# Cross attention of a decoder layer: probabilities turned in 32x32 blocks on VectorE, value products of two token tiles on sixteen 32x32 tiles of TensorE

## The chip, the core and the metric

The kernel runs on one core of a Trainium2 chip, as one launch. The metric is the device time of that launch in microseconds (us), smaller is better. The engines are named as in the profile: PE is TensorE (PEld its weight loads), DVE is VectorE, ACT is ScalarE, POOL is GpSimd and SP is SyncE, which issues the DMAs. Each engine works through its own queue in order.

## What is computed

A small encoder runs over a context of 77 positions, and its output is the memory of a decoder layer over 2 batches of 2048 tokens, width 512, 16 heads of 32. The decoder layer has causal self-attention, cross attention to the 77 positions and a feed-forward part of width 2048. All is fp32. The change touches cross attention:

```python
q = (xq @ wq.T + bq)          # 2048 tokens x 512, 16 heads of 32
scores = einsum('bhqd,bhkd->bhqk', q, k) / sqrt(32) + bias   # k: 77 positions
attn = softmax(scores, axis=-1)
out = einsum('bhqk,bhkd->bhqd', attn, v)                     # 32 values a head
y = y + out.reshape(B, T, 512) @ w_out.T + b_out
y = y + relu(ln(y) @ ff1.T + b1) @ ff2.T + b2
```

## The kernel before

The 4096 tokens are cut into 8 blocks of 512 tokens, and a block into four tiles of 128 tokens. The kernel first runs the encoder and the decoder's self-attention, and the cross attention of block 0 with it (`first_cross`, L888). The rest, whose first L1638 comes at 1652.9 us, is a loop (L1950) over the eight blocks. For each block it has 56 slots (`per`, L1500), and in each slot it issues two things in this order: one step of the cross attention of the *next* block (`next(side)`, the generator `cross`, L1727), then one step of this block's feed-forward part (`ff_slot`, L1704). The order of the work is thus written out by hand. The lists `plan[n]` hold what `cross` issues in slot n, and every engine takes its share of it in that order.

**Feed-forward part.** Slots 0 to 27 make the first product (`first_product`, L1629, matmuls L1638: eight PE instructions of 256 columns in each slot). Slots 28 to 55 make the second (`second_product`, L1658, matmuls L1667: sixteen PE instructions of 128 columns in a slot, and eight in each fourth slot). Both products use a scheme with seven products in place of eight, on two levels in the second. Its sums and differences of quarter matrices are made by DVE and POOL: `sums_h` (L1595, with `half_sum` L1584; the subtractions are recorded at L962, the additions at L1587 and L1605) runs four slots ahead of the product that reads them, in slots 24 to 51. Its product number j (order `TWO`, L1490) needs them in slots 28+4j and after; number 3 reads the sum called S4, number 4 the one called S3. Two parts of the product put their results together on DVE (L1676, and L1681 to L1683) and add them to y on POOL (L1687).

**Cross attention of a block** (`cross`). Slots 0 to 7: layer norm of the four tiles (`norm_stages`, L785: statistics on DVE L793 to L795 and POOL L796 and L797, centring on ACT L803, four transposes on PE L811, four copies on ACT L814). Slots 9 to 12: the queries (L1758). Then for each of the four tiles `attend_stages` (L824), begun in slots 13, 18, 23 and 28:

- `score` (L831), at once: sixteen products of 32 contracted rows with 77 positions (L836) into four PSUM banks; DVE then takes the maximum (L845) and subtracts it (L846), a pair for each bank, and writes the scores to SBUF.
- `exp` (L848), 2 slots on, on ACT (L849); `sums` (L851), 3 slots on, on DVE (L854, L855); `normalize` (L858), also 3 slots on, on POOL (L860).
- `turned` (L862), 7 slots on: sixteen PE transposes of 128 x 77 (L866) into four banks, each copied by ACT (L867).
- `times_v` (L869), 11 slots on: sixteen products with contraction 77 and 32 output rows (L874), four at a time on PE's four column groups, into one bank that ACT copies (L878).

After the second tile of a pair, `sums_o` (L1782) makes the differences for the output projection of that pair, and `o_product` (L1790, matmuls L1801) makes its seven products in slots 31 to 34 and 40 to 43; DVE adds each to y (L1805). A last layer norm (`n3`, same functions) begins in slots 35, 36, 44 and 45. An fp32 matmul is two MATMUL records and two weight loads in the profile, a transpose is one of each.

Four PSUM banks (0 to 3) go round in a ring among these cross steps (`bank`, L180); the feed-forward part has the other four. The probabilities of a tile lie in `prs[t % 2]`, 16 heads x 77 side by side; the two buffers are in `oT_all` and in `pts_all[5:8]`. The values of a batch lie once, 77 x 512, in a tile that was loaded before (`last_loads`, L1370, and `next_batch`, L1815).

Of the kernel before, what the change touches and what calls it, by code (L numbers as in the profile page):

```python
# [10 lines left out]
F32 = mybir.dt.float32  # L11
AF = mybir.ActivationFunctionType
ALU = mybir.AluOpType
# [4 lines left out]
P = 128  # L18
B, T, S, D = 2, 2048, 77, 512
H, HD, DFF = 16, 32, 2048  # L20
NC = D // P
# [33 lines left out]
def tile_encoder_decoder(ctx: ExitStack, tc: tile.TileContext, ins, out):  # L55
# [103 lines left out]
    with (  # L159
# [20 lines left out]
        def bank():  # L180

            ring.append(ring.pop(0))
            return psum[:, ring[-1], :]
# [6 lines left out]
        def rows4(r):  # L190
            return slice(r * HD, (r + 1) * HD)
# [626 lines left out]
        def q_group(o, w, nT, dst):  # L818
# [2 lines left out]
                nc.tensor.matmul(mm, w[:, c, :], nT[:, c, :], start=(c == 0), stop=(c == NC - 1))  # L821
            nc.vector.tensor_scalar(dst, mm, vec("dec_ca_in_b", o), SCALE, ALU.add, ALU.mult)

        def attend_stages(q, kTc, v, y, biased, pr, pts, place, w_o, bi=None):  # L824


            prh = pr.rearrange("p (h k) -> p h k", k=S)
            by_r = pr.rearrange("p (g r k) -> p g r k", r=HC, k=S)
            keep = {}

            def score():  # L831
# [14 lines left out]
                    nc.vector.tensor_tensor(d, s, mx[:, :, r, None].to_broadcast([P, NC, S]), ALU.subtract)  # L846

            def exp():  # L848
                nc.scalar.activation(pr, pr, AF.Exp)  # L849

            def sums():  # L851
                su = sm.tile([P, H], F32, name="csu", tag="csu", bufs=2)
# [108 lines left out]
        def minus(engine, out, a, b):  # L961
            engine.tensor_tensor(out, a, b, ALU.subtract)  # L962
# [385 lines left out]
        n2_sums, o_sums, vc, qT = [high[:, (4 + k) * D : (5 + k) * D] for k in range(4)], [], [], []  # L1348

        def big(i):  # L1350
            return vflat[:, i * TB * D : (i + 1) * TB * D]
# [375 lines left out]
        def cross(x):  # L1727
# [44 lines left out]
            plan[8].append(lambda: [sum_n(n, of_n2) for n in ("T1", "T2")])  # L1772
            plan[9].append(lambda: [sum_n(n, of_n2) for n in ("T3", "T4")])

            def of_o(t, name):
                if name[0] == "S":
                    i = int(name[1]) - 1
                    return o_sums[i // 2][:, ts(i % 2, TOK)]
                r, c = int(name[0]) - 1, int(name[1]) - 1
                return held["o", t + r]["oT"][:, ts(c, TOK)]  # L1780

            def sums_o(t):  # L1782
                s = {n: of_o(t, n) for n in ("S1", "S2", "S3", "S4", "11", "12", "21")}
                a21, a22 = (held["o", t + 1]["bank"][:, ts(c, TOK)] for c in range(2))
                minus(ve, s["S3"], s["11"], a21)
                minus(ve, s["S2"], a22, s["S3"])
                ve.tensor_tensor(s["S1"], s["21"], a22, ALU.add)
                minus(gp, s["S4"], s["12"], s["S2"])

            def o_product(t, j):  # L1790
                if j == 0:
                    held["out"] = bank(), bank()
                name, by, chain, fresh, to = ONE[j]
                a, mm = of_o(t, name), held["out"][chain][:, :TOK]
                if by[0] == "T":
                    w = next_w(2)
# [8 lines left out]
                ve.tensor_tensor(d, d, mm, ALU.add)  # L1805
# [1 line left out]
            for n, js in Q_SLOTS.items():  # L1807
                plan[n].append(lambda js=js: [q_product(j) for j in js])
            for n, js in O_SLOTS.items():
                t = 0 if n < 36 else 2  # L1810
                plan[n].append(lambda t=t, js=js: [o_product(t, j) for j in js])
            bias_1 = None
            if m == 0:

                def next_batch():  # L1815
                    nc.sync.dma_start(kTc, ckT_d[:, :, ts(b, S)])
                    nc.sync.dma_start(vc[0][:S, :], cv_d[:, b, :])

                plan[1].append(next_batch)

                spare = [y_of(x + 1, r) for r in range(HC)]
                bias_1 = [a[:, : NC * S].rearrange("p (g k) -> p g k", k=S) for a in spare]
                plan[3].append(lambda: bias_tile(prs[0].rearrange("p (h k) -> p h k", k=S), 2, P, S, 255))
                plan[5].append(lambda: [bias_tile(a, 2, P, S, 255 - P, r, HC) for r, a in enumerate(bias_1)])
            for t in range(TB):
                at = 13 + 5 * t
                y = lambda t=t: y_of(x, t)
                biased = m == 0 and t < 2
                fs = attend_stages(
                    lambda g, t=t: qT[g // 2][:, g % 2, ts(t, P)], kTc, vc[0][:S, :], y, biased, prs[t % 2],  # L1830
                    lambda g: pts_all[:S, g, :], place("xr"), wbt,
                    bias_1 if biased and t else None,
                )
                held["o", t] = fs[7]
# [159 lines left out]
```

## Time and profile before

| what | number |
|---|---|
| median of 3 runs | 2726.36 us (2726.09 to 2729.47) |
| profiled execution, first to last instruction | 2726.8 us |
| one block with cross attention, as in the loop (window 2215.2 to 2352.2 us of the trace) | 137.0 us |
| the last block, without cross attention (window 2626.2 to 2720.4 us) | 94.2 us |
| granted TensorE clock, mean | 0.997 of full speed |

The profiled execution has no time of its own beside its span: the span is 2726.8 us, and the median of the runs is 0.4 us below it. A page of the profile gives the busy time of each engine; the chain of waits is the work that ended last, followed back from the end. In the timeline, neighbouring instructions of one line are merged into a row (start, length, engine, line, count); in the windows, a row gives each engine's busy time in a stretch. A matmul's record runs on after the next one has started, so the cost of a burst on PE is read from its start to the next line's start.

### The profile page before, as it was taken

The numbers are of one execution on the slowest core, as the hardware profiler recorded it, in microseconds if no ns is written. First come the engines' busy times: TensorE is split into PE (matmuls) and PEld (weight loads), VectorE is DVE, ScalarE is ACT, GpSimd is POOL, SyncE is SP. The second block draws the span as 40 slices with busy tenths as digits, with TensorE's granted clock in tenths as the row PEclk, the third lists the DMA queues.
The fourth block names the chain that finished last, engine by engine and source line by source line (L and its number), as shares of the span: only waits on it lengthen the run. The fifth ranks groups of instructions, "written<-read, shape, count | busy, mean of one in ns | idle before, by whom it ended". The sixth has DMA issues, their size and how long they took to land.

```text
span 2726.8 us, 68267 instructions
## 1 busy us (share of the span) xinstructions
PE 2708.1 (99%) x26606; PEld 2217.9 (81%) x26606; DVE 1839.9 (67%) x5445; ACT 1537.0 (56%) x2978; POOL 1002.4 (37%) x844
## 2 busy tenths in 40 slices
PE   9999999999999999999999999999999999999998
PEld 6678877777876677777777777898989898989898
DVE  4776688888885677788888783646464746464645
ACT  3554567777786547667777784444444444444431
POOL 2612235500300513322300203455556565656456
PEclk9999999999999999999999999999999999999999
DMA  8724355511213522343311206565657565656465
GB/s 242 213 92 135 126 155 164 168 50 43 67 45 89 143 76 72 111 133 98 126 50 35 79 19 220 171 214 173 213 171 239 168 216 170 218 166 219 151 224 185
DMA packets 296277, 385.10 MB, mean 141 GB/s; under 512 B 41184, under 2 KB 165648, under 8 KB 295826
## 3 DMA queue, kind: packets, MB, share of 16 engines
q1 hardware_dynamic: 295954, 380.73, 44.1%
q8 instruction: 211, 3.46, 0.5%
q14 instruction: 112, 0.92, 0.1%
HBM read 334.15 MB, written 46.47 MB: 140 GB/s over the span
## 4 chain that ended last, share of the span: by engine, by line
PE 95%; DVE 1%; ACT 1%; DMA 1%; POOL 1%; issue 1%; SPq 0%; DVEq 0%; POOLq 0%; ACTq 0%
PE psum L427 18%; PE psum L1638 14%; PE psum L1667 13%; PE psum L375 11%; PE psum L456 9%; PE psum L1134 8%; PE psum L1801 3%; PE psum L1758 3%; PE psum L1049 3%; PE psum L866 2%; PE psum L836 1%; PE psum L874 1%; PE psum L590 1%; PE psum L811 1%; PE psum L239 1%; PE psum L215 1%
## 5 line engine op out<-in xcount | busy, mean ns | idle before, releaser
L406 ACT ACTIVATE pp<-pp,nm 128x128 f32<-128x128 f32 (+15 forms) x512 | 611.8, 1200 | 28.6 <-DVE nm L401 27.8
L384 DVE TENSOR_SCALAR_CACHE_REDUCE pp<-psum 128x512 f32<-128x512 f32 (+3 forms) x1024 | 556.2, 591 | 51.3 <-PE psum L375 49.7
L434 ACT COPY pts<-psum 128x512 f32<-128x512 f32 x714 | 384.1, 594 | 312.6 <-PE psum L427 265.6
L427 PE MATMUL psum<-ident,pp 128*128 128x128 f32 x4352 | 530.4, 277 | 4.7 <-ACT nT L310 4.0
L427 PEld LDWEIGHTS psum<-ident,pp 128*128 128x128 f32 x4352 | 474.0, 141 | 55.7 <-DVE pp L384 21.4
L375 PE MATMUL psum<-kT,q 32*128 32x512 f32 (+3 forms) x2560 | 336.5, 559 | 2.5 <-DVE q L217 1.0
L456 PEld LDWEIGHTS psum<-pts,vv 128*32 128x32 f32 x8704 | 226.4, 110 | 127.4 <-DVE pp L384 55.4
L1667 PE MATMUL psum<-pp 128*128 128x128 f32 x2560 | 304.5, 276 | 1.9 <-POOL pp L962 1.6
L1667 PEld LDWEIGHTS psum<-pp 128*128 128x128 f32 x2560 | 296.3, 192 | 8.6 <-issue 2.8
L432 DVE COPY pts<-psum 128x512 f32<-128x512 f32 x374 | 245.2, 685 | 82.6 <-PE psum L427 80.3
L456 PE MATMUL psum<-pts,vv 128*32 128x128 f32 x8704 | 279.6, 276 | 0.8 <-DVE mx L391 0.3
L962 POOL TENSOR_TENSOR pp<-pp 128x512 f32<-128x512 f32 x159 | 212.8, 1356 | 111.0 <-DMA pp<-in_dec_ff_wT_dram 50.6
L1638 PE MATMUL psum<-vv,pp 128*128 128x256 f32 x1024 | 236.2, 381 | 0.0
L375 PEld LDWEIGHTS psum<-kT,q 32*128 32x128 f32 x2560 | 146.3, 183 | 107.1 <-issue 41.3
L1638 PEld LDWEIGHTS psum<-vv,pp 128*128 128x128 f32 x1024 | 190.3, 190 | 25.8 <-issue 0.5
L391 DVE CUSTOM_DVE_ANT_0 pp<-psum,bias 128x256 f32<-128x256 f32 (+1 forms) x512 | 196.0, 411 | 19.7 <-PE psum L375 19.7
L1651 DVE TENSOR_TENSOR kT<-kT,psum 128x512 f32<-128x512 f32 x96 | 65.8, 686 | 191.6 <-PE psum L1638 191.4
L1654 ACT ACTIVATE kT<-kT,vecs 128x256 f32<-128x256 f32 x192 | 86.9, 501 | 156.6 <-DVE kT L1651 155.9
L1638 PE MATMUL psum<-nT,pp 128*128 128x256 f32 x768 | 174.1, 380 | 0.5 <-DVE oT L471 0.5
L1638 PEld LDWEIGHTS psum<-nT,pp 128*128 128x128 f32 x768 | 144.2, 190 | 20.8 <-issue 1.4
L1675 ACT COPY oT<-psum 128x128 f32<-128x128 f32 x56 | 15.0, 268 | 238.9 <-PE psum L1667 238.9
L494 POOL TENSOR_TENSOR oT<-rirows,oT 128x512 f32<-128x512 f32 x30 | 38.4, 1280 | 293.6 <-DMA rirows<-rec 181.7
(272 smaller groups left out, 4110.6 us busy)
## 6 DMA issues: line engine op xcount, KB each, us to landing
pp<-w_d SPq DMA_DIRECT2D x520, 256.0 KB
pp<-in_dec_ff_wT_dram SPq DMA_DIRECT2D x112, 256.0 KB
bias<-tzg SPq DMA_DIRECT2D x128, 128.0 KB
pp<-wo_d SPq DMA_DIRECT2D x56, 256.0 KB
wqk<-in_dec_sa_in_wT_dram SPq DMA_DIRECT2D x52, 256.0 KB
wqk<-sa_q SPq DMA_DIRECT2D x84, 128.0 KB
vv<-in_enc_ff_wT_dram SPq DMA_DIRECT2D x8, 1024.0 KB
xr<-in_x_dram SPq DMA_DIRECT2D x32, 256.0 KB
```

The source lines that it names most:

```text
L375: nc.tensor.matmul(banks[r][:, : kn * P], q[rows4(r), ts(t, P)], kT[rows4(r), g, k0 * P : (k0 + kn) * P], start=True, stop=True,)
L384: nc.vector.tensor_scalar(p[:, k0 : k0 + far], s[:, :far], 1.0, None, ALU.mult, ALU.max, accum_out=st["mx"][:, r, c : c + 1],)
L391: nc.vector.tensor_tensor_reduce(p[:, k0 + far : i + 1], s[:, far:kn], near[:, 2 - (kn - far) :], 1.0, LOWEST, ALU.add, ALU.max, accum_out ...
L406: nc.scalar.activation(p, p, AF.Exp, bias=nm, accum_out=to)
L427: nc.tensor.transpose(pt[:, ts(x, P)], state[n]["p"][r][:, k], ident)
L432: nc.vector.tensor_copy(pts[:, : len(load), :], pt[:, :w])
L434: nc.scalar.copy(pts[:, : len(load), :], pt[:, :w])
L456: nc.tensor.matmul(ot[rows4(r)], vv[:, k, ts(g * HC + r, HD)], got.pop((n, k, r)), start=k == k0 and (whole or not begun), stop=k == k1 - ...
L962: engine.tensor_tensor(out, a, b, ALU.subtract)
L1134: nc.tensor.matmul(mm[:, ts(f, TOK)], left[:, c, ts(f, P)], right[:, c, :], start=c == 0, stop=c == 1,)
L1638: nc.tensor.matmul(mm[:, ts(f, TOK)], a[:, c, ts(f, P)], b[:, c, :], start=fresh and f == 0 and c == 0, stop=c == 1, skip_group_check=True,)
L1667: nc.tensor.matmul(psum[:, bank_i, ts(col, P)], lhs[:, c, :], w[:, c, :], start=fresh and k in (0, 3) and c == 0, stop=c == 3, skip_group_ ...
```

## The change

Transposes on PE and their copies on ACT go away. VectorE turns the normalised probabilities in place, each 32x32 block by itself (`blocks_turned`). For that each head gets 96 columns instead of 77 (three blocks of 32), and both probability buffers move to `oT_all`; `mixed` of the feed-forward part moves to `pts_all[5:8]`. After the turn, a block has 32 positions on 32 partitions and 32 queries on its columns, and the four groups of 32 partitions hold the four groups of 32 queries. The products with the values are therefore made for each of the four row groups, with the values lying four times (`v4`, 32 positions on each group, three chunks of positions, the rest of the last chunk zero). `times_v` now does two tiles at once: 4 groups of heads x 3 chunks x 4 row groups x 4 column groups = 192 matmuls with 32 contracted rows, 32 output rows and 64 columns, into four banks; two ACT copies bring the result into the old order, one for each tile.

The slots move: scores begin in 13, 17, 31 and 35 (13, 18, 23 and 28 before), the turn comes 6 slots after a tile's score, the products of a pair 8 slots after its second tile's score (25 and 43), the output products in 27 to 30 and 45 to 48, the last norms in 31, 32, 49 and 50. `first_cross` uses `attend_stages` as before.

```diff
+        def heads_of(pr):
+            return pr.rearrange("p (h k) -> p h k", h=H)[:, :, :S]
...
-            prh = pr.rearrange("p (h k) -> p h k", k=S)
-            by_r = pr.rearrange("p (g r k) -> p g r k", r=HC, k=S)
+            prh = heads_of(pr)
+            by_r = prh.rearrange("p (g r) k -> p g r k", r=HC)
...
-                nc.scalar.activation(pr, pr, AF.Exp)
+                nc.scalar.activation(prh, prh, AF.Exp)
...
-        prs = [oflat[:, : H * S], pts_all[:, 5:8, :].rearrange("p a k -> p (a k)")[:, : H * S]]
+        KC = 3
+        prs = oflat.rearrange("p (a x) -> p a x", a=2)
+        v4 = pts_all[:, :KC, :]
...
-            t = sb.tile([P, MB], F32, name="q", tag="q", bufs=3)
-            nc.sync.dma_start(t[:S, :], cv_d[:, 0, :])
-            vc.append(t)
...
-        O_SLOTS = {at + k: js for at in (31, 40) for k, js in enumerate(((0, 1), (2, 3), (4, 5), (6,)))}
+        SCORE_AT = (13, 17, 31, 35)
+        OUT_AT = (27, 45)
+        NORM_AT = (31, 32, 49, 50)
+        O_SLOTS = {at + k: js for at in OUT_AT for k, js in enumerate(((0, 1), (2, 3), (4, 5), (6,)))}
...
-        mixed = oflat[:, H * S : H * S + 12 * P].rearrange("p (k n) -> p k n", n=P)
+        mixed = pts_all[:, 5:8, :].rearrange("p a (k n) -> p (a k) n", n=P)
...
+            def load_v(batch):
+                for a in range(P // RB):
+                    for c in range(KC):
+                        n = min(RB, S - c * RB)
+                        nc.sync.dma_start(v4[a * RB : a * RB + n, c, :], cv_d[c * RB : c * RB + n, batch, :])
+
+            def first_v():
+                nc.gpsimd.memset(v4[:, KC - 1, :], 0.0)
+                load_v(0)
+
+            def blocks_turned(t):
+                pr = prs[:, t % 2]
+                nc.vector.transpose(pr, pr)
+
+            def times_v(t):
+                for _ in range(P // RB):
+                    bank()
+                pT = prs.rearrange("p a (h c q) -> p a h c q", h=H, c=KC)
+                for g in range(NC):
+                    for c in range(KC):
+                        for a in range(P // RB):
+                            for r in range(HC):
+                                h = g * HC + r
+                                nc.tensor.matmul(
+                                    psum[rows4(r), a, ts(g, 2 * RB)], v4[ts(a, RB), c, ts(h, HD)],
+                                    pT[ts(a, RB), :, h, c, :], start=(c == 0), stop=(c == KC - 1),
+                                )
+                got = psum[:, : P // RB, : NC * 2 * RB].rearrange("p a (g x q) -> p x g a q", g=NC, x=2)
+                for x in range(2):
+                    oT = place("xr")()
+                    nc.scalar.copy(oT.rearrange("p (g a q) -> p g a q", g=NC, q=RB), got[:, x])
+                    held["o", t + x] = oT, got[:, x]
+                sums_o(t)
...
-                minus(ve, s["S3"], s["11"], a21)
-                minus(ve, s["S2"], a22, s["S3"])
-                ve.tensor_tensor(s["S1"], s["21"], a22, ALU.add)
+                f = {n: s[n].rearrange("p (g a q) -> p g a q", g=2, q=RB) for n in ("S1", "S2", "S3", "11", "21")}
+                minus(ve, f["S3"], f["11"], a21)
+                minus(ve, f["S2"], a22, f["S3"])
+                ve.tensor_tensor(f["S1"], f["21"], a22, ALU.add)
...
+            if x == 1:
+                plan[10].append(first_v)
...
-                    nc.sync.dma_start(vc[0][:S, :], cv_d[:, b, :])
+                    load_v(b)
...
             for t in range(TB):
-                at = 13 + 5 * t
+                at = SCORE_AT[t]
...
-                if t % 2:
-                    fs = fs[:5] + (lambda t=t, f=fs[5]: [f(), sums_o(t - 1)],)
-
-                for k, f in zip((0, 2, 3, 3, 7, 11), fs):
-                    plan[at + k].append(f)
+                fs = fs[:4] + (lambda t=t: blocks_turned(t),)
+                for k, f in zip((0, 2, 3, 3, 6), fs):
+                    plan[at + k].append(f)
+                if t % 2:
+                    plan[at + 8].append(lambda t=t: times_v(t - 1))
                 fs = norm_stages(y, "n3", bo, place("xt"), lambda t=t: nTt[:, :, ts(t, P)])
-                at = (35, 36, 44, 45)[t]
+                at = NORM_AT[t]
```

More of the change, by code (lines that the diff above doesn't have):

```diff
@@ L1345, in tile_encoder_decoder @@
         oflat = oT_all.rearrange("p a q -> p (a q)")
-        prs = [oflat[:, : H * S], pts_all[:, 5:8, :].rearrange("p a k -> p (a k)")[:, : H * S]]
+        KC = 3
+        prs = oflat.rearrange("p (a x) -> p a x", a=2)
+        v4 = pts_all[:, :KC, :]
         kTc = pts_all[:, 4, : NC * S].rearrange("p (c k) -> p c k", k=S)
-        n2_sums, o_sums, vc, qT = [high[:, (4 + k) * D : (5 + k) * D] for k in range(4)], [], [], []
+        n2_sums, o_sums, qT = [high[:, (4 + k) * D : (5 + k) * D] for k in range(4)], [], []
         def big(i):
@@ L1779, in of_o @@
                 r, c = int(name[0]) - 1, int(name[1]) - 1
-                return held["o", t + r]["oT"][:, ts(c, TOK)]
+                return held["o", t + r][0][:, ts(c, TOK)]
             def sums_o(t):
                 s = {n: of_o(t, n) for n in ("S1", "S2", "S3", "S4", "11", "12", "21")}
-                a21, a22 = (held["o", t + 1]["bank"][:, ts(c, TOK)] for c in range(2))
-                minus(ve, s["S3"], s["11"], a21)
-                minus(ve, s["S2"], a22, s["S3"])
-                ve.tensor_tensor(s["S1"], s["21"], a22, ALU.add)
+                a21, a22 = (held["o", t + 1][1][:, 2 * c : 2 * c + 2] for c in range(2))
+                f = {n: s[n].rearrange("p (g a q) -> p g a q", g=2, q=RB) for n in ("S1", "S2", "S3", "11", "21")}
+                minus(ve, f["S3"], f["11"], a21)
+                minus(ve, f["S2"], a22, f["S3"])
+                ve.tensor_tensor(f["S1"], f["21"], a22, ALU.add)
                 minus(gp, s["S4"], s["12"], s["S2"])
@@ L1809, in cross @@
             for n, js in O_SLOTS.items():
-                t = 0 if n < 36 else 2
+                t = 0 if n < OUT_AT[1] else 2
                 plan[n].append(lambda t=t, js=js: [o_product(t, j) for j in js])
+            if x == 1:
+                plan[10].append(first_v)
             bias_1 = None
@@ L1822, in cross @@
                 bias_1 = [a[:, : NC * S].rearrange("p (g k) -> p g k", k=S) for a in spare]
-                plan[3].append(lambda: bias_tile(prs[0].rearrange("p (h k) -> p h k", k=S), 2, P, S, 255))
+                plan[3].append(lambda: bias_tile(heads_of(prs[:, 0]), 2, P, S, 255))
                 plan[5].append(lambda: [bias_tile(a, 2, P, S, 255 - P, r, HC) for r, a in enumerate(bias_1)])
             for t in range(TB):
-                at = 13 + 5 * t
+                at = SCORE_AT[t]
                 y = lambda t=t: y_of(x, t)
```

4 lines of the change are left out of this document (1 added, 3 removed).

## The prediction

> **What bounds the kernel now.** First the page: busy times, then the chain of waits.
>
> ```profile
> span 2726.8 us, 68267 instructions
> PE 2708.1 (99%) x26606; PEld 2217.9 (81%) x26606; DVE 1839.9 (67%) x5445; ACT 1537.0 (56%) x2978; POOL 1002.4 (37%) x844
> ...
> PE 95%; DVE 1%; ACT 1%; DMA 1%; POOL 1%; issue 1%; SPq 0%; DVEq 0%; POOLq 0%; ACTq 0%
> ```
>
> PE never rests and holds 95% of the chain, so time taken off PE counts until another engine is late. But these are averages. I therefore cut out one block (2215.2 to 2352.2 us) in the windows view, then its two halves: slots 0 to 27 and 28 to 55.
>
> ```profile
> core 0: us, PE busy (x) PEld busy (x) DVE busy (x) ACT busy (x) POOL busy (x), PEclk, DMA share, GB/s
> 2215.20:2352.20 137.00, 137.00 (x1082) 124.50 (x1081) 76.37 (x149) 57.68 (x123) 77.71 (x67) 1.00 0.59 192
> 2215.20:2287.20 72.00, 72.00 (x490) 62.35 (x488) 31.82 (x62) 39.89 (x84) 31.04 (x29) 1.00 0.47 151
> 2287.20:2352.20 65.00, 65.00 (x596) 62.15 (x593) 44.55 (x87) 17.80 (x39) 46.67 (x39) 1.00 0.73 239
> ```
>
> In the first half DVE and POOL are idle more than half of the time; in the second they are busy 44.6 and 46.7 of 65.0 us. The timeline of the last block, which has no cross attention to stretch it, shows what happens there when PE goes faster: PE itself waits, for sums of DVE and POOL (bracket: idle before, and for whom).
>
> ```profile
> 2694.65 4.07 PE L1667 MATMUL psum<-pp 128*128 128x128 f32 x32 [0.27 <-DVE pp L962]
> 2699.13 3.84 PE L1667 MATMUL psum<-pp 128*128 128x128 f32 x32 [0.40 <-POOL pp L962]
> 2704.16 1.05 PE L1667 MATMUL psum<-pp 128*128 128x128 f32 x7 [1.19 <-POOL pp L962]
> ```
>
> So the second half is close to a second limit, and what the change moves there decides.
>
> **What leaves PE.** PE's timeline in that block; a burst costs from its start to the next line's start.
>
> ```profile
> 2274.39 1.99 PE L1638 MATMUL psum<-vv,pp 128*128 128x256 f32 x8
> 2276.31 1.08 PE L874 MATMUL psum<-pts,q 77*32 77x128 f32 x32
> 2277.32 1.99 PE L1638 MATMUL psum<-nT,pp 128*128 128x256 f32 x8
> 2279.16 1.91 PE L866 MATMUL psum<-ident,pts 128*77 128x128 f32 x16
> 2280.90 1.89 PE L1638 MATMUL psum<-nT,pp 128*128 128x256 f32 x8
> 2282.63 3.62 PE L1638 MATMUL psum<-vv,pp 128*128 128x256 f32 x16
> ...
> 2292.12 2.06 PE L866 MATMUL psum<-ident,oT 128*77 128x128 f32 x16
> 2294.02 1.95 PE L1667 MATMUL psum<-pp 128*128 128x128 f32 x16
> ```
>
> Undisturbed, eight L1638 take 1.73 (2280.90 to 2282.63). Transposes: 1.74 plus 0.11 before them (2277.32 + 1.73 to 2279.16), 1.85; once 1.90, a wait of 0.16. Values: 1.01 plus 0.19 before them, 1.2. Four tiles: 4 x 1.85 + 0.16 + 4 x 1.2 = **12.4 us** a block.
>
> **What comes to PE.** Two bursts a block of 192 fp32 matmuls, two instructions each (L874 has 32 for sixteen matmuls): 384 instructions, 24 on each tile. No row has row and column tiling together. Nearest are the encoder's value products, 77 columns on four column groups; the second fence is the same view, cut to the burst's first 0.04 us.
>
> ```profile
> 126.81 0.74 PE L645 MATMUL psum<-pp 77*32 77x77 f32 x32
> 127.48 1.33 PE L637 MATMUL psum<-ident,pp 77*77 77x77 f32 x16
> ```
> ```profile
> 126.81 0.27 PE L645 MATMUL psum<-pp 77*32 77x77 f32 x4
> ```
>
> Less a last instruction of about 0.25, 32 start within 0.49: 0.0156 apart, so each of four tiles takes one every 0.063. L874 likewise: (1.08 - 0.27)/31 = 0.026, or 0.104 a tile for 128 columns. Between them lie 51 columns and 0.041; 64 columns give 0.052. Sixteen tiles at once: 24 x 0.052 = 1.25. The second fence shows that four tiles begin within 0.27 - 0.25 = 0.02, some 0.007 apart, so the sixteenth starts 0.1 later. Entry and exit as now: 1.2 - 32 x 0.026 = 0.37. Sum 1.72; I take 1.75 a pair, **3.5 a block**. From above: if each instruction, not each matmul, needs those 0.007, 384 of them take 2.7 (3.1 with the rest); if only four tiles run at once, 96 x 0.052 = 5.0 (5.4). From below, nothing can take less than 24 passes. I take the low end, as L645 and L874 are limited by their tile's stream and not by starts. PE alone thus saves 12.4 - 3.5 = 8.9 us a block.
>
> **What goes to DVE.** Four turns of 1536 columns.
>
> ```profile
> L484 DVE STREAM_TRANSPOSE rt<-ri x30: 211/211/214, 52.7 to 1535.6; 128x32 f32<-128x32 f32 x30
> ...
> L854 DVE TENSOR_REDUCE csu<-oT 128x16 f32<-128x1232 f32 x2 | 2.9, 1436 | 2.3 <-ACT oT L849 2.3
> ```
>
> By the reduce's rate a turn costs 1.436 x 1536/1232 = 1.79; I take **1.78**. Below, half of that, as no row with one SBUF input runs so; above, 48 blocks at 0.211, 10.1. Between: if 0.06 of the 0.211 grows with each block, about 3.1. The reduce is nearest in size. [...]
>
> **What is late next.** Tile 2's score moves from slot 23, where DVE is idle, to 31, tile 3's from 28 to 35, and the norm of tiles 0 and 1 comes between. I walk the queues in these slots with:
>
> ```profile
> 2286.18 1.13 PE L836 MATMUL psum<-pts,bias 32*128 32x77 f32 x32
> 2287.24 2.05 PE L1667 MATMUL psum<-pp,kT 128*128 128x128 f32 x16
> ...
> 2338.84 0.60 PE L811 MATMUL psum<-ident,q 128*128 128x128 f32 x4
> 2339.27 1.95 PE L1667 MATMUL psum<-pp,kT 128*128 128x128 f32 x16
> ```
> ```profile
> 2287.33 0.48 DVE L845 TENSOR_REDUCE cmx<-psum 128x4 f32<-128x308 f32 x1 [0.93 <-PE psum L836]
> ...
> 2291.00 1.28 DVE L1587 TENSOR_TENSOR pp<-kT 128x512 f32<-128x512 f32 x2
> ...
> 2299.59 0.25 DVE L855 RECIPROCAL cri<-csu 128x16 f32<-128x16 f32 x1
> 2299.76 0.36 DVE L1681 TENSOR_TENSOR oT<-psum,oT 128x256 f32<-128x256 f32 x1
> 2300.02 2.25 POOL L860 TENSOR_TENSOR pts<-pts,cri 128x1232 f32<-128x1232 f32 x1 [2.34 <-DVE cri L855]
> ...
> 2300.70 0.74 DVE L1805 TENSOR_TENSOR vv<-vv,psum 128x256 f32<-128x256 f32 x2
> 2301.36 3.13 DVE L962 TENSOR_TENSOR pp<-pp,kT 128x512 f32<-128x512 f32 x2
> 2302.23 1.72 POOL L962 TENSOR_TENSOR pp<-pp 128x512 f32<-128x512 f32 x1
> ```
> ```profile
> L793 DVE BATCH_NORM_STATS2 bnst<-vv 128x6 f32<-128x512 f32 x8 | 5.5, 683 | 0.0
> ...
> L796 POOL TENSOR_TENSOR crs<-crs,mhalf 128x1 f32<-128x1 f32 x8 | 5.3, 662 | 0.3 <-DVE crs L795 0.3
> ...
> L803 ACT ACTIVATE xt<-vv,crs 128x512 f32<-128x512 f32 x5 | 4.1, 815 | 1.9 <-POOL crs L797 1.9
> L814 ACT ACTIVATE nT<-psum,vecs 128x128 f32<-128x128 f32 x16 | 6.0, 456 | 4.4 <-PE psum L811 4.4
> ```
>
> So: a score costs PE 1.06 and reaches DVE after 1.15; DVE's eight operations take 3.67 (2287.33 to 2291.00), its three additions to `mixed` 0.94 (2299.76 to 2300.70), a sum of two SBUF tiles 0.64 alone and 1.57 while POOL works (3.13 for two): 0.93 of waiting. A feed-forward slot costs 1.79 or 0.89, four transposes 0.43.
>
> - *Slot 35, score 3.* PE comes there 1.06 + 0.89 + 3 x 1.79 + 0.43 = 7.7 after score 2 began. Its fourth bank is that of tile 0's norm; the copies out of it stand in ACT's queue behind tile 1's centring, which waits for tile 1's statistics, which stand on DVE behind score 2: 1.15 + 3.67 + 0.94 + 1.0 (statistics), POOL 1.0, ACT 0.82 + 4 x 0.456, three hand-overs of 0.18 (2299.84 to 2300.02): 10.9. **PE waits 3.2.**
> - *Slot 40, the S4 half.* From score 3 on, DVE does 1.15 + 3.67 + 0.94, two S4 halves 1.28, the turn 1.78, a half 0.64, an addition 0.41, sums 1.68, the last half 0.64, one wait for POOL 0.93: 13.1. PE needs it after 1.06 + 0.89 + 0.43 + 3 x 1.79 + 0.89 + 0.89 = 9.5. **3.6.**
> - *Slot 42.* POOL does `normalize` of tile 3 first (2.25), then the two differences for S4 (1.27 each), with a DVE half before each: 6.1 against PE's 0.89 + 1.79 + 0.89 = 3.6. **2.5.**
>
> Together 9.3 a block. The rest costs nothing: ACT loses sixteen copies and was not late; the values' 12 DMAs a batch go ahead of a ring of sixteen loaded weight tiles, which covers them; the first half has room for turns and products (without that cover, 2 x 1.78 a block).
>
> **Sum.** -12.4 + 3.5 + 9.3 = +0.4 a block; seven blocks, +2.8 on a span of 2726.8, whose median is 2726.36: **2729 us**. The waits are known to about 2 us a block: 2715 to 2743.
>
> **The rivals.**
> 1. *The backlog is absorbed.* PE that waits once gives DVE time; if two of the three waits are really one, 4 a block remain: -4.9 x 7, 2692; if none remains, -62, 2664. For it: today DVE is full in slots 28 to 33 and PE does not wait. Against: the waits of the last block above. Chance 0.22.
> 2. *PE does not run sixteen tiles at once* (slower): at 3.1 a pair +2.7 a block, 2748; at 5.4 +7.3, 2780. It decides from 1.55 a pair, where the sum above is zero. 0.11 and 0.06.
> 3. *The turn is dearer*: at 3.1 it adds 1.3 to the second wait and as much for tile 3, +2.6 a block, 2747; at 10.1, +16.6, 2845. 0.11 and 0.02.
> 4. [...] 0.02.
>
> **How the numbers follow.** The forecast has 0.46. A measurement here tells 0.2%, 5.5 us, from no change. Of the 0.46 I put 0.10 below that band, 0.20 in it, 0.16 above. Faster: 0.10 + 0.22 = 0.32; same 0.20; slower 0.16 + 0.17 + 0.13 + 0.02 = 0.48. The range 2695 to 2760 leaves out half of the first rival (0.11) and the dear ends of the others (0.10).
>
> **What would show it.** PE's timeline: a values burst of 384 in about 1.75. DVE: a turn of 1.78. PE's waits: some 9 us a block, ended by ACT L814 at score 3 and by L962 of DVE and POOL in slots 40 to 42. If DVE's scores end before PE needs the banks, the walk is wrong and the first rival right; a longer burst is the second, a longer turn the third.

## The result, and the profile after

| kernel | median | ratio to before (95% interval) |
|---|---|---|
| before | 2726.23 us (4 runs, 2725.19 to 2729.47) | |
| changed | 2862.81 us (4 runs, 2862.08 to 2866.58) | 1.0496 (1.0481 to 1.0511) |

The change makes the kernel 5% slower, 134.2 us from span to span (2861.0 against 2726.8), or 19.2 us on average in each of the seven blocks with cross attention. The prediction was 2729 us with a range of 2695 to 2760. The page of the changed kernel:

```profile
PE 2739.1 (96%) x30638; PEld 2243.4 (78%) x30638; DVE 1902.9 (67%) x5473; ACT 1482.4 (52%) x2866; POOL 999.3 (35%) x845
...
q8 instruction: 242, 3.96, 0.6%
...
PE 86%; DVE 5%; issue 4%; POOL 2%; ACT 2%; DMA 1%; SPq 0%; DVEq 0%; POOLq 0%; ACTq 0%
```

PE was to lose work, and it is busy 31 us longer; it also rests now (96% in place of 99%). In the chain stands 4% of "issue": time in which the engine waited for nothing that the profile shows. PE's waits over the whole program name the line:

```profile
PE psum L1803 <- issue: 56.5, 29, 3.1
PE psum L839 <- ACT nT L814: 20.3, 7, 2.9
PE psum L1672 <- POOL pp L965: 11.1, 16, 1.2
PE psum L1672 <- DVE pp L965: 9.6, 8, 1.4
```

L1803 are the new value products (L839 the scores, L1672 the second feed-forward product, L814 the copies behind the norm's transposes; three to five lines lower than before). The columns are total idle time, number of waits, longest. The three rows below the first are the waits that the prediction had. The first it did not have. One block (2294.09 to 2448.24 us) in the windows view, and its two bursts in PE's timeline:

```profile
2294.09:2448.24 154.15, 140.80 (x1658) 127.61 (x1657) 84.44 (x153) 49.93 (x107) 77.52 (x67) 0.94 0.54 172
```
```profile
2353.90 1.67 PE L1803 MATMUL psum<-oT,pts 32*32 32x64 f32 x146
2356.61 1.50 PE L1803 MATMUL psum<-oT,pts 32*32 32x64 f32 x128 [1.04 <-issue]
2360.08 1.81 PE L1803 MATMUL psum<-oT,pts 32*32 32x64 f32 x110 [1.97 <-issue]
2361.82 3.43 PE L1643 MATMUL psum<-nT,pp 128*128 128x256 f32 x8
2365.09 1.89 PE L1643 MATMUL psum<-vv,pp 128*128 128x256 f32 x8
...
2387.98 0.45 PE L839 MATMUL psum<-pts,bias 32*128 32x77 f32 x6
2391.33 1.34 PE L839 MATMUL psum<-pts,bias 32*128 32x77 f32 x26 [2.90 <-ACT nT L814]
2392.60 2.08 PE L1672 MATMUL psum<-pp 128*128 128x128 f32 x8
...
2395.32 7.41 PE L1672 MATMUL psum<-pp 128*128 128x128 f32 x64
2404.08 2.94 PE L1672 MATMUL psum<-pp 128*128 128x128 f32 x24 [1.35 <-DVE pp L965]
...
2410.64 1.98 PE L1803 MATMUL psum<-oT,pts 32*32 32x64 f32 x178
2415.71 1.84 PE L1803 MATMUL psum<-oT,pts 32*32 32x64 f32 x128 [3.10 <-issue]
2419.18 1.38 PE L1803 MATMUL psum<-oT,pts 32*32 32x64 f32 x78 [1.63 <-issue]
2420.49 4.02 PE L1672 MATMUL psum<-pp 128*128 128x128 f32 x24
2424.36 1.89 PE L1841 MATMUL psum<-wbig,xr 128*128 128x256 f32 x8
```

Three things matter here. A burst takes 7.92 us (2353.90 to 2361.82) and 9.85 us (2410.64 to 2420.49), not 1.75. It comes in three parts, the middle one of **exactly 128 records** both times, with PE idle between them; the first may have 146 or 178. And the product behind a burst is slow too: eight L1643 take 3.27 (2361.82 to 2365.09) in place of the 1.73 of before.

This suggests what the idle time is. 128 matmul records with their 128 weight loads are 256 instructions. The page's instruction queue (q8: packets, MB, share of 16 DMA engines) moved 3.96 MB in 242 packets, 16.4 KB each. The page of before has 211 packets and 68267 instructions, this one 76148: 31 packets more for 7881 instructions more, 254 each. The DMA view, cut to the first burst (2353.9 to 2361.8 us), has three packets; the row above them is the busy share of the DMA engines in tenths, in 40 slices of 0.2 us:

```profile
DMA  9750045889200000000300000000000000003000
q8 instruction: 3, 0.05, 2.3%
```

Three packets share 0.023 x 16 x 7.9 = 2.9 us of one DMA engine, 0.97 each, and they come with pauses between them: behind the first third of the row nothing moves but two packets. The same view in windows of 1 us puts the three at 2354.4, 2357.8 and 2361.2 us, 3.4 us apart, and the second and third part of the burst begin 2.2 and 2.3 us after a packet. Both times these parts begin 3.47 us apart (2356.61 and 2360.08, 2415.71 and 2419.18). The other twelve bursts look the same: a middle part of exactly 128 records in each, 122 to 250 records before the first gap, and 3.47 to 3.75 us (once 4.02) between the starts of the later parts. So the theory:

**S (supply).** PE's instructions come in packets of 256, one in about 3.5 us, and a burst of 768 runs through what is there in 1.5 to 2 us and then waits, twice. **Rivals: A**, the array: sixteen 32x32 tiles are slow in themselves, by their stream or their switching. **F**: the packets wait behind the weights' transfers. **W**: the waits of the new schedule are the loss, and the bursts only show it.

### The profile page after: what moved, and what is told of

Same layout as the page of the kernel before. It is cut to its first block, busy times and chain, and to the rows that moved or that the text cites. A ratio compares the mean times of both kernels' runs of the same rounds, so it can differ in the third digit from the quotient of the medians.

```text
span 2861.0 us, 76148 instructions
## 1 busy us (share of the span) xinstructions
PE 2739.1 (96%) x30638; PEld 2243.4 (78%) x30638; DVE 1902.9 (67%) x5473; ACT 1482.4 (52%) x2866; POOL 999.3 (35%) x845
## 3 DMA queue, kind: packets, MB, share of 16 engines
q8 instruction: 242, 3.96, 0.6%
## 4 chain that ended last, share of the span: by engine, by line
PE 86%; DVE 5%; issue 4%; POOL 2%; ACT 2%; DMA 1%; SPq 0%; DVEq 0%; POOLq 0%; ACTq 0%
PE psum L427 17%; PE psum L1643 14%; PE psum L375 10%; PE psum L456 9%; PE psum L1672 8%; PE psum L1137 8%; PE psum L1841 3%; PE psum L1763 3%; PE psum L1803 2%; PE psum L1052 2%; PE psum L839 1%; POOL pp L965 1%; PE psum L590 1%; PE psum L239 1%; DVE cmx L848 1%
## 5 line engine op out<-in xcount | busy, mean ns | idle before, releaser
L1672 PE MATMUL psum<-pp 128*128 128x128 f32 x2560 | 329.9, 288 | 21.7 <-POOL pp L965 11.1
L1672 PEld LDWEIGHTS psum<-pp 128*128 128x128 f32 x2560 | 318.8, 203 | 30.4 <-POOL pp L965 14.4
L1643 PE MATMUL psum<-vv,pp 128*128 128x256 f32 x1024 | 235.8, 382 | 1.3 <-DVE kT L1656 1.3
L1643 PEld LDWEIGHTS psum<-vv,pp 128*128 128x128 f32 x1024 | 194.0, 192 | 28.4 <-DVE kT L1656 1.7
L1643 PE MATMUL psum<-nT,pp 128*128 128x256 f32 x768 | 187.1, 398 | 0.5 <-DVE oT L471 0.5
L1643 PEld LDWEIGHTS psum<-nT,pp 128*128 128x128 f32 x768 | 151.4, 200 | 23.8 <-issue 1.2
L1680 ACT COPY pts<-psum 128x128 f32<-128x128 f32 x56 | 14.8, 265 | 252.0 <-PE psum L1672 251.7
```

Source lines behind the costliest of these rows:

```text
L1643: nc.tensor.matmul(mm[:, ts(f, TOK)], a[:, c, ts(f, P)], b[:, c, :], start=fresh and f == 0 and c == 0, stop=c == 1, skip_group_check=True,)
L1672: nc.tensor.matmul(psum[:, bank_i, ts(col, P)], lhs[:, c, :], w[:, c, :], start=fresh and k in (0, 3) and c == 0, stop=c == 3, skip_group_ ...
```

## The experiments

Each run stood beside runs of the kernel before on the same chip: 2724.80 us for the first four, 2728.63 for the next four, 2728.91 for the last two (the version with free slots and the second one in four pieces). Only the two versions in three pieces were run five times; every other time is that of a single run. The diffs are against the changed kernel where nothing else is said. Where one block of a run is shown it is the shortest of that run; the longest, leaving out the first, is 3 to 8 us longer. A matmul of the code is two records, so a burst is 192 matmuls and 384 records; where an expectation counts 48 matmuls a piece it means those of the code.

### The same products in four pieces: two versions

```diff
-                    plan[at + 8].append(lambda t=t: times_v(t - 1))
+                    for g in range(NC):
+                        plan[at + FROM + g].append(lambda t=t, g=g: times_v(t - 1, (g,)))
...
-        OUT_AT = (27, 45)
-        NORM_AT = (31, 32, 49, 50)
+        OUT_AT = (29, 47)
+        NORM_AT = (33, 34, 51, 51)
+        FROM = 7
```

`times_v` makes the products of one group of heads at each call, and the copies with the last.

> The value products of a pair of tiles are cut into four pieces of 48 matmuls (one group of heads each) that stand in four slots behind one another, 7 to 10 slots after the pair's second score; the copies and the output products move two slots later, the norms two. Theory S (supply: PE's sequencer holds some 150 of these matmuls with their weight loads ahead, and a burst of 384 runs it dry twice): each piece is within the store, has no idle time put down to issue, and takes 0.6 to 1.1 us, so 2.4 to 4.4 us a pair in place of 7.9 and 9.9, and the half clock behind the bursts goes; 7 blocks x (17.8 - 7) = 75 us less, about 2785 us (2765 to 2805). Rival A (the array: 32x32 tiles are slow in themselves, whatever stands ahead of them): four pieces take together the 8 to 10 us of the one, the time stays at 2850 to 2870. Rival W (the waits of the new schedule are the loss): the time stays too, and the waits at scores and output products grow.

2818.41 us, above the range of S. In this version the third score takes over banks in which output products are still being added, so part of the first pair's output products is lost. A second version has the output products in 28 and 46 and the norms in 32, 33, 50 and 51, and computes all:

> Four pieces of 96 records (one group of heads each) in the slots of the changed kernel: pieces in 24 to 27 and 42 to 45, output products one slot later (28 and 46), norms one later (32, 33, 50, 51), scores as they were. Unlike the first version in four pieces, the output products' sums are all there before the third score takes over their banks. Theory S: as the first one, 2818 us within 15, since the order of the instructions differs by little; what is left above the kernel before is the turn that comes late for the first piece, the scores' waits and those of the last products. Rival A (the array): 2850 to 2870.

2831.36 us, in the range. PE's waits in the first version, and then in the second:

```profile
PE psum L1805 <- DVE oT L1793: 15.7, 14, 3.1
...
PE psum L1805 <- issue: 10.2, 14, 1.6
```
```profile
PE psum L1805 <- DVE oT L1793: 29.5, 14, 3.1
PE psum L811 <- DVE oT L849: 27.9, 7, 4.0
PE psum L1805 <- issue: 7.1, 10, 1.4
```

The issue time of the value products (L1805 here) falls from 56.5 us to 10.2 and 7.1 with the same 10752 instructions. That speaks for S and against A. The time came down only by 44 and 31 us, not by 75: the first piece now stands one slot sooner and waits for the turn (L1793), 15.7 and 29.5 us in all, and in the second version the norm's transposes (L811) wait 27.9 us for DVE's scores, so the waits of the schedule grew.

### Half the columns

```diff
-                                    psum[rows4(r), a, ts(g, 2 * RB)], v4[ts(a, RB), c, ts(h, HD)],
-                                    pT[ts(a, RB), :, h, c, :], start=(c == 0), stop=(c == KC - 1),
+                                    psum[rows4(r), a, 2 * g * RB : (2 * g + 1) * RB], v4[ts(a, RB), c, ts(h, HD)],
+                                    pT[ts(a, RB), 0, h, c, :], start=(c == 0), stop=(c == KC - 1),
...
```

> Each of the value matmuls takes 32 columns in place of 64: the products of a pair's second tile are left out, and its output is a copy of the first tile's. Number and order of the instructions stay. Theory S (supply): the bursts keep their 8 to 10 us and their idle time put down to issue, the time stays within 2845 to 2870 us. Rival A (the array's stream sets the burst): half the columns take half the time of a burst, 9 us less in each of 7 blocks, about 2800 us.

2855.97 us, in the range of S. Half of the array's stream saves 7 us, not 60.

```profile
2348.99 2.62 PE L1803 MATMUL psum<-oT,pts 32*32 32x32 f32 x273
2354.35 1.40 PE L1803 MATMUL psum<-oT,pts 32*32 32x32 f32 x111 [2.75 <-issue]
```

One gap is missing here, as 273 records (17 + 2 x 128) lay ready, and the other is longer. This burst lasts from 2348.99 to 2355.68, 6.7 us. It is the only one of the fourteen with two parts; over all of them the issue time is 61.4 us, not less than 56.5. Within a part, 273 records take 2.62 us: 9.6 ns each with 32 columns, and 1.67/146 = 11.4 with 64. So the pace too is set for the most part by something other than the stream.

### One chunk of positions

```diff
-                    for c in range(KC):
+                    for c in range(1):
...
-                                    pT[ts(a, RB), :, h, c, :], start=(c == 0), stop=(c == KC - 1),
+                                    pT[ts(a, RB), :, h, c, :], start=True, stop=True,
```

> Only the first of the three chunks of 32 keys is multiplied: 128 value matmuls a pair in place of 384, two thirds of the value products are left out. Theory S (supply): 128 matmuls are within the store of some 150, so the burst falls to less than a third: 1.2 to 2.0 us (the first piece of the whole burst took 1.67 for 146) with no idle time put down to issue inside it; 7 x (17.8 - 3.4) = 100 us less, and some 10 more with the half clock: 2750 us (2740 to 2775). Rival A (the array): a third of the work takes a third of the time, 2.6 to 3.3 us a burst, 2780 us.

2736.08 us, 4 us under the range of S. A third of the products takes less than a fifth of the burst's time, and PE waits for no instruction in the burst, here and in 12 of the other 13 (one has a gap of 1.5 us). The rows are those of the timeline, then one block in the windows view:

```profile
2281.99 1.47 PE L1803 MATMUL psum<-oT,pts 32*32 32x64 f32 x128
2283.39 1.99 PE L1643 MATMUL psum<-nT,pp 128*128 128x256 f32 x8
2285.22 1.89 PE L1643 MATMUL psum<-vv,pp 128*128 128x256 f32 x8
...
2308.12 0.45 PE L839 MATMUL psum<-pts,bias 32*128 32x77 f32 x6
...
2312.51 1.35 PE L1672 MATMUL psum<-pp 128*128 128x128 f32 x8
...
2314.51 8.38 PE L1672 MATMUL psum<-pp 128*128 128x128 f32 x64
...
2330.75 1.47 PE L1803 MATMUL psum<-oT,pts 32*32 32x64 f32 x128
```
```profile
2222.18:2358.83 136.65, 131.08 (x1146) 119.40 (x1145) 85.81 (x153) 49.68 (x107) 77.60 (x67) 0.99 0.62 193
```

1.40 us a burst (2281.99 to 2283.39). The eight L1643 behind it take 1.83: no slow product now. This block, with all else as the changed kernel has it, lasts 136.65, as long as the 137.0 of before, and the whole run is 11 us above its kernel before. So almost all of the 134 us lies with the two thirds that were left out, and W cannot be the main loss.

### Whole bursts, other slots

```diff
-        SCORE_AT = (13, 17, 31, 35)
-        OUT_AT = (27, 45)
-        NORM_AT = (31, 32, 49, 50)
+        SCORE_AT = (13, 16, 25, 29)
+        OUT_AT = (31, 40)
+        NORM_AT = (35, 36, 44, 45)
```

> The bursts stay whole; scores start in slots 13, 16, 25 and 29 in place of 13, 17, 31 and 35, output products in 31 and 40 in place of 27 and 45, norms in 35, 36, 44 and 45, so that more slots lie between a burst and what needs it. Theory S (supply): the bursts stay at 8 to 10 us with their idle time put down to issue; only the waits of PE at the third and fourth score (2.9 us) and at the second pair's output products (2.7 us) go: 7 x 5.6 = 39 us less at most, 2823 us (2815 to 2850). Rival W (the waits are the loss): 2740 to 2780 us.

2857.01 us: neither theory's number. PE's waits tell why:

```profile
PE psum L1803 <- issue: 57.9, 28, 3.1
PE psum L1841 <- DVE vv L1845: 22.2, 10, 2.7
```

The old waits went, as expected, and the output products (L1841) now wait for DVE instead, 22 us in all. The bursts kept their 58 us of issue time. The waits were moved and not removed, so this run alone does not decide on W.

### No weights from DRAM

```diff
-                nc.sync.dma_start(dst, src)
+                if fed[0] <= len(w_ring):
+                    nc.sync.dma_start(dst, src)
```

> The changed kernel, but weight tiles are brought in only for the first sixteen places of the ring; later products take those again, so the weights' transfers of all blocks are left out (and the products have wrong weights). Theory S as it stands (the store is refilled in its own time): bursts stay at 8 to 10 us with 1 to 3 us of issue idle time twice in each; 2855 to 2865 us. Rival F (the refill waits behind the weights' transfers, which fill the DMA engines to 40 to 60% in these stages): gaps below 1 us, a burst of 5 to 6 us, some 8 us a block less: about 2800 us.

2852.23 us, 3 us under the range of S. A stretch of 154 us in the windows view (the last two columns are the DMA engines' busy share and GB/s), and the waits:

```profile
2294.00:2448.00 154.00, 142.43 (x1662) 129.48 (x1661) 85.55 (x154) 50.09 (x108) 77.95 (x70) 0.94 0.06 17
```
```profile
PE psum L1804 <- issue: 48.2, 26, 2.3
```

The DMA engines are busy 6% of the time in place of 54%, and the issue time falls only from 56.5 to 48.2. F explains at most some 8 us. The later parts come no sooner on a nearly empty path: in one burst of this run (2405.01 to 2413.80 us in PE's timeline) they begin at 2408.74 and 2412.48, 3.74 us apart.

### All 128 rows: no row tiles

```diff
-                                    psum[rows4(r), a, ts(g, 2 * RB)], v4[ts(a, RB), c, ts(h, HD)],
-                                    pT[ts(a, RB), :, h, c, :], start=(c == 0), stop=(c == KC - 1),
+                                    psum[rows4(r), a, ts(g, 2 * RB)], v4[:, c, ts(h, HD)],
+                                    pT[:, :, h, c, :], start=(c == 0), stop=(c == KC - 1),
```

> Each value product takes all 128 partitions as its rows in place of a block of 32 (so each sum runs over the four blocks, which isn't what the reference wants); number and order of the instructions and their columns stay, but the array is no longer cut into rows. Theory S (supply counts instructions, not tiles): idle time put down to issue stays, 1 to 3 us twice in a burst, burst 8 to 11 us, 2850 to 2880 us. Rival A (the sixteen 32x32 tiles are at fault): no such gaps; 384 records at 13 to 17 ns make 5 to 6.5 us, about 2800 to 2815 us.

2841.16 us, 9 us under the range of S and far above that of A. Timeline of a burst:

```profile
2341.87 2.25 PE L1803 MATMUL psum<-oT,pts 128*32 128x64 f32 x145
2344.80 1.99 PE L1803 MATMUL psum<-oT,pts 128*32 128x64 f32 x128 [0.68 <-issue]
2348.27 1.77 PE L1803 MATMUL psum<-oT,pts 128*32 128x64 f32 x111 [1.48 <-issue]
2349.97 2.00 PE L1643 MATMUL psum<-nT,pp 128*128 128x256 f32 x8
```

The tiles are four times as high, 128 records take 1.99 us in place of 1.50, and the gaps stand at the same counts. The parts begin again 3.47 us apart (2344.80, 2348.27), and the burst takes 8.1 in place of 7.92: its length is set by the packets, not by what the array does between them. That excludes A for the gaps. Why it is 22 us faster than the changed kernel shows in the clock (columns behind the busy times: PEclk, DMA share, GB/s), for the 3.43 us behind the burst, first the changed kernel, then this one:

```profile
2361.82:2365.25 3.43, 3.43 (x13) 2.84 (x10) 1.17 (x3) 1.07 (x2) 1.19 (x2) 0.57 0.00 0
```
```profile
2349.97:2353.40 3.43, 3.43 (x21) 3.05 (x17) 2.16 (x5) 1.44 (x3) 1.18 (x2) 1.00 0.11 34
```

After the gaps of the 32x32 bursts the granted clock is 0.57 of full speed, after those of this kernel 1.00. The eight L1643 behind the first burst of a block take 3.11 to 3.58 us in all seven blocks of the changed kernel, and 1.83 in the block shown here (2349.97 to 2351.80). So the changed kernel has a second loss, in the products behind its bursts. It goes with the gaps (with one chunk and no gap they take 1.83 too), but gaps alone do not bring it, as this run shows.

### One chunk and other slots

The two edits of "one chunk", and

```diff
-        SCORE_AT = (13, 17, 31, 35)
-        OUT_AT = (27, 45)
-        NORM_AT = (31, 32, 49, 50)
+        SCORE_AT = (13, 15, 26, 27)
+        OUT_AT = (30, 41)
+        NORM_AT = (36, 37, 45, 46)
```

> One chunk of keys in place of three (two thirds of the value products left out, as in the run before with one chunk: 2736.1 us), and the slots of the version in three pieces: scores in 13, 15, 26, 27, output products in 30 and 41, norms in 36, 37, 45, 46. If what that run still lost to the kernel before is PE's waits at the third and fourth score and at the second pair's output products, as the prediction had them (9.3 us a block), most of them go here: 7 x 4 to 7 x 6 us less, 2695 to 2708 us. If the rest was lost elsewhere (turn, ACT, the cost of a burst), the time stays at 2730 to 2740 us.

2706.86 us, 29 less than with the old slots. One block:

```profile
2205.63:2337.53 131.90, 130.02 (x1147) 117.90 (x1145) 83.51 (x153) 49.58 (x107) 77.71 (x67) 1.00 0.63 200
```

Idle time 1.88 us in place of 5.57 (136.65 - 131.08). PE is busy 7.0 us less than in the block of before (137.0). So with a third of the value products the change does take time off PE, and in the changed kernel's slots the predicted waits ate it.

### All products, in three pieces

```diff
+        PIECES = 3
+        FROM = (23, 36)
...
-                    plan[at + 8].append(lambda t=t: times_v(t - 1))
+                    for i in range(PIECES):
+                        plan[FROM[t // 2] + i].append(lambda t=t, i=i: times_v(t - 1, i))
```

with the scores, output products and norms in the slots of the version before, and the loops of `times_v` cut accordingly.

> All value products, in their order, cut into three pieces of 128 records a pair of tiles (64 matmuls of the code, two records each) in three slots behind one another (23 to 25 and 36 to 38); scores start in slots 13, 15, 26, 27, output products in 30 and 41, norms in 36, 37, 45, 46. Theory S (supply): a piece of 128 takes what the single chunk took, about 1.5 us, so 4.5 us a pair, without idle time put down to issue inside it. Against the run with a single chunk (2736.1 us) that is 7 x 2 x 2 x 1.5 = 42 us more, less what the slots save in waits (up to 7 x 5 = 35 us): 2745 us (2725 to 2780), near the kernel before. Rival A (the array): three pieces cost together the 8 to 10 us of the burst: above 2820 us.

2768.56 us (5 runs), ratio to before 1.0145 (1.0131 to 1.0159). In the range, but with idle time that was not expected:

```profile
2288.34 1.48 PE L1805 MATMUL psum<-oT,pts 32*32 32x64 f32 x128
...
2291.67 0.39 PE L1805 MATMUL psum<-oT,pts 32*32 32x64 f32 x32
2292.90 1.16 PE L1805 MATMUL psum<-oT,pts 32*32 32x64 f32 x96 [0.83 <-issue]
```

The first piece runs through; the next, 3.3 us later, runs dry after 32 records, and the third (at 2295.92) after 23. Piece and slot are 272 instructions in 3.3 us, a little more than a packet in 3.5. A free slot between the pieces should mend it (diff against the version just shown):

```diff
-        SCORE_AT = (13, 15, 26, 27)
-        OUT_AT = (30, 41)
-        NORM_AT = (36, 37, 45, 46)
-        FROM = (23, 36)
+        SCORE_AT = (13, 15, 28, 30)
+        OUT_AT = (32, 46)
+        NORM_AT = (44, 45, 50, 51)
+        FROM = (23, 39)
...
-                        plan[FROM[t // 2] + i].append(lambda t=t, i=i: times_v(t - 1, i))
+                        plan[FROM[t // 2] + 2 * i].append(lambda t=t, i=i: times_v(t - 1, i))
```

> The version in three pieces again, but with a free slot between each piece and the next (23, 25, 27 and 39, 41, 43); scores in 13, 15, 28, 30, output products in 32 and 46, norms in 44, 45, 50, 51. PE's instructions are seen to arrive in packets of 16,384 bytes, one in 3.4 to 3.5 us while a burst runs, and 128 value matmuls with their weight loads lie between two gaps. Theory S in this form (one packet of 256 instructions in 3.4 us): a piece of 256 instructions every 5 us leaves time for the packet, the issue idle time of the version without free slots (4.2 us a block) goes, 7 x 4.2 = 29 us less than its 2768.6, if no wait takes its place: 2740 us (2728 to 2758). Rival G (the idle time belongs to the change from one kind of product to the other, so to each piece): it stays, 2762 us or more.

2752.02 us (5 runs), ratio to before 1.0085 (1.0072 to 1.0099). One piece with what follows it, and one block:

```profile
2296.80 1.48 PE L1805 MATMUL psum<-oT,pts 32*32 32x64 f32 x128
2298.20 0.70 PE L1645 MATMUL psum<-vv,pp 128*128 128x256 f32 x2
2299.65 1.56 PE L1645 MATMUL psum<-vv,pp 128*128 128x256 f32 x6 [0.75 <-issue]
```
```profile
2229.96:2368.55 138.59, 135.93 (x1658) 122.51 (x1657) 84.50 (x153) 50.20 (x108) 78.06 (x67) 1.00 0.62 191
```

The three pieces of this burst stay whole, 1.40 us each (as from 2296.80 to 2298.20), and the value products' issue time is 3.6 us in the program (11.4 without the free slots). Part of it moved on to the feed-forward products behind the pieces, as the last row of the timeline shows: with them the issue time falls from 17.4 to 8.5 us. The packet rate thus foretold the direction; of the 29 us expected, 16.5 came. PE is busy 135.93 us in this block, 1.07 less than before, but 2.66 us of waits outweigh it; over all seven blocks PE is busy 971.4 us against 973.3 before. This was the best version with all products, and it does not beat the kernel before. If all its waits could go, 2 us (by all blocks) to 7.5 us (seven times this block) would be gained, at most 0.3%: an estimate from these rows, not tried.

## Why the prediction was wrong

It failed at one term, "What comes to PE", 1.75 us a pair, and it put at nothing what hangs on that term: the half clock behind the bursts.

- **The burst, 3.5 a block.** Measured 7.92 + 9.85 = 17.8 in the block shown; the mean of all fourteen bursts is 8.9. Two errors lie in it. First the pace: the prediction let sixteen tiles share the stream, 0.052/16 = 0.003 us for each record, and excluded the other end, 0.007 for each instruction started, because L645 and L874 go by their streams. Without any gap 128 records take 1.40 us, 0.011 each, so 4.2 a pair, 4.9 more a block than the term; half the columns changed that little. Sixteen tiles gave 0.011 us a record where the four tall tiles of the run over 128 rows gave 0.0155, and not a quarter of it; what sets the 0.011 (starting, or weight loads, which come with every record) no run here tells apart. Second, and larger (17.8 - 8.4 = 9.4 a block): it asked only how fast PE works, not how fast it gets its instructions. The bursts that it quoted have 16 to 32 records and show no gap; but 768 instructions in 1.75 us could have been held against the instruction queue on the page of before, one packet in 12.9 us on average:

```profile
q8 instruction: 211, 3.46, 0.5%
```

- **The half clock.** Not in the prediction. In the block shown: 3.27 - 1.73 behind the first burst, 3.87 (2420.49 to 2424.36, at a granted clock of 0.70) - 2.68 behind the second, 2.7 together, and some 1.4 behind the wait at score 3 (2392.60 to 2395.32, at a granted clock of 0.50, in place of 0.89 + 0.43).
- **The waits, 9.3.** The mechanism was right, place by place and with the engines named. Score 3: 3.56 (2387.98 to 2392.60, less 1.06) against 3.2; with one chunk 3.3 (2308.12 to 2312.51). Slots 40 to 42: 2395.32 to 2410.64, 15.32 for 104 records of L1672 that take 11.6 undisturbed (6.5 x 1.79), so 3.7 against 3.6 + 2.5; with one chunk 4.6 (2314.51 to 2330.75). DVE and POOL were late by 1.5 to 2.4 us less than the walk through their queues had it; why, no run shows. With the better slots all but 1.9 of the idle time goes.
- **What leaves PE, 12.4.** Right in the main: with it, the measured bursts of 2 x 1.40 and waits of 3.3 + 4.6, the block with one chunk comes to 137.0 - 12.4 + 2.8 + 7.9 = 135.3; it took 136.65. With the better slots, and 1.9 of idle time in place of the 7.9, it comes to 129.3 and took 131.9. So 1.4 to 2.6 us a block of it did not show, and no run tells where they went.
- **The turn, 1.78.** Right; 28 of them, in ns:

```profile
L1792 DVE STREAM_TRANSPOSE oT<-oT x28: 1764/1766/1778, 1717.1 to 2719.2; 128x1536 f32<-128x1536 f32 x28
```

- **The sum.** -12.4 + 17.8 + 7.3 + 4.1 = +16.8 for the block shown, which took 154.15 - 137.0 = 17.15. The other six blocks with cross attention are 18.6 to 20.7 us longer than before; the mean of all seven is 19.2.
- **The rivals.** The first, a backlog that is absorbed, is out: 7.3 of the 9.3 us of waits came. The second, PE's slowness, had the sign and by far too small a price (2780 at most). Nearest in time was the dear end of the third, 2845 us by a turn of 10.1: a coincidence, as the turn took 1.77. The fourth, with its chance of 0.02, rested on a least time between the starts of two instructions that no run shows; here records start 0.011 us apart (128 in 1.40 us) and then stop at the gaps.

The kernel before has no such wait: the feed-forward part of a slot, matmul records with their weight loads, needs 16 instructions in 1.73 us (eight L1638) or 32 in 1.79 (sixteen L1667), and PE has no wait put down to issue. In the two bursts shown a gap is 1.04 to 3.10 us.

The granted clock is 0.50 behind the 2.90 us of idle time at score 3 (2392.60 to 2395.32), and 0.57 on average in the 3.43 us behind the first burst shown, which has gaps of 1.04 and 1.97 us with 1.5 us of work between them. With 128 rows it is 1.00 behind both bursts of the block (2349.97 to 2353.40 and 2407 to 2412), though 0.82 from 2397.3 to 2407, most of which is the second burst. Why the first keeps the full clock behind it, with 2.2 us of gaps in place of 3.0 and taller tiles, no run here explains.

## What to carry to other kernels

Count instructions before time: in these bursts PE got 256 of them (128 matmul records with their weight loads) in about 3.5 us, and what it had ahead was one to two such packets (122 to 273 records before the first gap). A change that replaces few long matmuls by many short ones is to be held against that. Here 272 instructions in 3.3 us ran dry, and 288 in 5 us ran through for the most part. Spread such products over slots with long matmuls, and count about 0.01 us for a record, as tiles of 32x32 took 9.6 ns with 32 columns and 11.4 with 64. And when PE is made faster beside engines that are nearly full, walk their queues: the waits found that way were right within 2 us a block in sum.

## What the runs showed of the hardware

- The later parts of a burst begin 3.47 to 3.75 us apart in the changed kernel (once 4.02). They begin 3.74 us apart in the burst quoted from the run without weights (DMA engines 6% busy in place of 54%), and 3.47 and 3.75 in the two bursts of the block shown with tiles of 128 rows (2344.80 and 2348.27, 2402.23 and 2405.98). In the first burst shown of the changed kernel the packets come 3.4 us apart, and a packet itself occupies a DMA engine for 0.97 us; what the rest of the time is stays open.
- With 64 columns in 32x32 tiles the array's stream is not the limit: half the columns moved the pace from 11.4 to 9.6 ns a record.
- Behind the first burst shown of the changed kernel, with gaps of 1.04 and 1.97 us, the granted clock was 0.57 over 3.43 us; behind the burst of full-height tiles shown, with gaps of 0.68 and 1.48 us, it was 1.00. What makes the difference stays open.
